# Four graph layers on one core: seven half-size products in layers 1 and 2 as well, the neighbour mask in PSUM, and a new issue order

## The chip, the cores and the metric

The kernel runs on one core of a Trainium2 chip. The metric is the device time of one execution in microseconds (us). The kernel before has a median of 3687.53 us over three runs (3678.21 to 3694.46).

## The reference

64 independent graphs of 256 nodes with 512 features each pass through four layers. Each layer normalises the rows, clips them at zero and adds its result to `x`:

```python
for layer in range(4):
    h = maximum(layernorm(x), 0)
    x = x + gnn[layer](h, adj)

# layer 0: q, k (64 wide), v = h @ W;  w = softmax_n(sum_m((q k^T / 8) * adj));   w * v
# layer 1 (8 heads of 64): f = h @ W + b;  e_self, e_neigh = f . a_self, f . a_neigh
#          d = leaky_relu(e_self[i] + e_neigh[j], 0.2) - 1e10 * (1 - adj);  relu(softmax_j(d) @ f)
# layer 2 (8 heads of 64): p = h @ Wp + b;  relu(tanh(adj * (p C^T p^T)) @ p)
# layer 3: q, k, v (512 wide) = h @ W;  w = softmax_n(sum(q * (adj @ k)) * mask / sqrt(512));   w * v
```

All data are float32.

## The kernel before, in words

A graph's 256 nodes lie as two chunks of 128 partitions (node `2p + c` on partition `p`). For each graph about a hundred *steps* are defined by name in `graph(b)`; a step issues from one to sixteen instructions. The class `Plan` sorts the steps of all graphs by `b * PERIOD + TIMES[name]` (the first nine and the last eight graphs have tables of their own, `FIRST` and `LAST`, and the steps that prepare weights have `WEIGHTS`), records them in this order, and ties each instruction to the one recorded before it on its engine. So every engine works in a fixed order, across some six graphs that are under way at once. Only the order on each engine counts; the tables' times are in us, but nothing waits for a time.

Buffers come from pools by `take` and go back by `done`, first in, first out, also in recorded order: eight PSUM banks, 6 `xt`, 3 `adj`, 6 `at`, 2 `all` (twice as large as the others), 2 `negt`, 2 `half`, and 12 `big` ones, to which 4 are added once the weights are ready.

A layer goes like this. Row sums and squares give `rstd` and `shift` (`sx` on ACT, `rs` on DVE, `pw` and `sh` on POOL; layer 0 uses `st`, the statistics instruction of DVE, line 982, in place of sums). `hn` on ACT makes the normalised rows. To transpose them, `sq` transposes 32 x 32 squares on DVE (line 912), `sw` writes them to memory (line 1029), and `ht` reads them back in the other order (line 917), both issued from the SP queue. Then come the products.

- Layers 0 and 3 (`products`, line 1060) make one product of [256 x 512] by [512 x 2w] from **seven products of half size**. POOL makes four sums of blocks of the transposed rows (`sa`, `sb`, lines 1065 to 1073), PE seven products of two matmuls each (line 1081), and DVE adds their results from PSUM (`add_to`, line 1095; `part_of_score`, line 1135). Their weight differences `t0_s`, `t3_s` are made once.
- Layers 1 and 2 use plain products (`rows`, line 906): `fa` and `fb` with 272 and 256 columns, 4 matmuls for each chunk; `xp` with 512 columns. DVE adds the bias and takes the results out of PSUM (`fae` with the copy `ec`, `fbe`, `xe`; lines 1246 to 1257 and 1436).
- Layer 1 then broadcasts the rows `e_neigh` and `e_self` to all partitions through memory (`er`, `enes`, lines 1271 to 1276), takes the maximum of `e_neigh` over the neighbours (`max0` to `max3`, 16 instructions, line 1288; the mask `neg` turned `adj` into -1e10 where there is no edge, line 944), broadcasts it (`mr`, `mb`), and makes the attention for pairs of heads: `ea` (ACT, line 1327), `eg` adds the mask (POOL, line 1334), `eb` subtracts the maximum (DVE, line 1340), `ex` (ACT, line 1346), `po` (PE, line 1358), `eh` and `su` sum up (POOL line 1367, PE line 1381).
- Layer 2: the transposed projection times C (`xc`, line 1461), scores in pairs of banks (`ps`, line 1487), `tv` (DVE, line 1511), `ta` (ACT, line 1518), `py` (PE, line 1501).
- Layer 3: `agg` (PE, line 1550), its copy `ga` (line 1559), then the seven products `g1` to `g7`. `add3` (DVE, line 1570) adds the weighted rows to `x`, and `store` sends them.

## Time and profile before

| | |
|---|---|
| median of three runs | 3687.53 us |
| the profiled execution, its own time | 3695.39 us |
| its span, first to last instruction | 3693.3 us |
| mean granted clock of PE | 0.985 |
| PE busy (matmuls) | 3494.9 us, 95% |
| DVE busy | 3251.5 us, 88% |
| ACT busy | 2415.6 us, 65% |
| POOL busy | 1623.2 us, 44% |
| busy share of the DMA engines | 69% of 16, 785 MB |

In a group of instructions, the line, engine, operation, tiles and shapes come first, then the count; after the first bar the busy time in us and the mean of one in ns; after the second bar the engine's idle time just before such instructions and what ended it. One f32 product of the program stands as two matmul records. In a list of waits each line has the waiting engine and line, what it waited for, the total in us, the number of times and the longest.

### The profile page before, as it was taken

To read this page: it belongs to the slowest core of one execution; us is meant where nothing else is said; L and a number is where in the kernel's file an instruction comes from. 1 tells how busy PE (TensorE), PEld (TensorE's weight loads), DVE (VectorE), ACT (ScalarE), POOL (GpSimd) and SP (SyncE) were. 2 spreads that over 40 slices of the span, in tenths; PEclk is the share of its full clock that TensorE was granted. 3 is DMA by queue.
4 is the path that set the end of the run, shared out by engine and by line. 5 is a ranking of instruction groups with operands and counts; after the bars stand their busy time and mean duration, and the time that the engine had idled before them with its cause. 6 is when DMAs were issued, how large, how long until landed. Compare 5 with 4: busy or idle time off the path is not lost.

```text
span 3693.3 us, 57357 instructions
## 1 busy us (share of the span) xinstructions
PE 3494.9 (95%) x16322; PEld 2031.4 (55%) x16322; DVE 3251.5 (88%) x8558; ACT 2415.6 (65%) x5381; POOL 1623.2 (44%) x1811
## 2 busy tenths in 40 slices
PE   6889999999999999999999999999999999998988
PEld 3555555555555555555555555555555555555544
DVE  6789898999898999999999899899899999898866
ACT  2567666667667667667766767667666766656654
POOL 2454444454444454444454444354444444343441
PEclk8899999999999999999999999999999999999999
DMA  6667666776776777777777777777677777676643
GB/s 192 196 217 218 211 213 199 223 222 217 222 220 211 224 223 221 227 228 217 222 229 211 223 224 212 219 234 214 216 231 219 221 224 221 198 215 190 210 149 120
DMA packets 967467, 785.00 MB, mean 213 GB/s; under 512 B 788912, under 2 KB 859120, under 8 KB 942576
## 3 DMA queue, kind: packets, MB, share of 16 engines
q1 hardware_dynamic: 967152, 781.34, 69.0%
q8 instruction: 132, 2.16, 0.2%
q14 instruction: 183, 1.50, 0.1%
HBM read 511.12 MB, written 270.01 MB: 211 GB/s over the span
## 4 chain that ended last, share of the span: by engine, by line
DVE 32%; PE 24%; DMA 19%; ACT 10%; issue 7%; SPq 6%; POOL 2%; DVEq 0%; ACTq 0%; POOLq 0%
DMA big<-sq_d 9%; DMA sq_d<-big 9%; PE bank L1081 8%; PE bank L906 7%; DVE big L912 6%; DVE big L1095 5%; ACT big L1416 5%; DVE big L1340 4%; PE bank L1358 3%; SPq L917 2%; SPq L1179 2%; DVE big L1163 2%; ACT big L974 2%; DVE bank L1135 2%; PE bank L1487 2%
## 5 line engine op out<-in xcount | busy, mean ns | idle before, releaser
L906 PE MATMUL bank<-w_s,big 128*128 128x256 f32 (+2 forms) x3072 | 956.1, 462 | 48.7 <-DMA big<-sq_d 42.6
L906 PEld LDWEIGHTS bank<-w_s,big 128*128 128x128 f32 x3072 | 604.3, 199 | 435.1 <-issue 281.9
L1081 PE MATMUL bank<-t_s,big 128*128 128x320 f32 (+1 forms) x1536 | 610.1, 528 | 39.2 <-POOL big L1065 31.2
L996 POOL TENSOR_TENSOR rstd<-rstd,power 128x2 f32<-128x2 f32 x256 | 178.9, 699 | 1053.6 <-DVE rstd L990 999.2
L1334 POOL TENSOR_TENSOR big<-big,negt 128x1024 f32<-128x1024 f32 x256 | 605.8, 2389 | 21.6 <-ACT big L1327 18.0
L1288 DVE CUSTOM_DVE_ANT_0 junk<-all,adj 128x256 f32<-128x256 f32 x1024 | 485.9, 475 | 32.2 <-DMA all<-er_d 1.5
L1346 ACT ACTIVATE big<-big 128x1024 f32<-128x1024 f32 x256 | 258.8, 1051 | 389.6 <-DVE big L1340 388.6
L1367 POOL TENSOR_TENSOR half<-big 128x512 f32<-128x512 f32 x256 | 325.2, 1291 | 424.9 <-ACT big L1346 288.9
L1009 ACT ACTIVATE big<-xt,shift,rstd 128x512 f32<-128x512 f32 x512 | 383.4, 805 | 171.4 <-POOL shift L1002 169.2
L912 DVE STREAM_TRANSPOSE big<-big 128x512 f32<-128x512 f32 x640 | 472.6, 774 | 19.4 <-ACT big L1009 18.9
L1327 ACT ACTIVATE big<-all,ec 128x256 f32<-128x256 f32 x1024 | 428.1, 494 | 80.2 <-DMA all<-er_d 76.4
L1095 DVE TENSOR_TENSOR big<-bank,big 128x320 f32<-128x320 f32 (+1 forms) x704 | 393.9, 568 | 35.4 <-PE bank L1081 19.9
L1081 PEld LDWEIGHTS bank<-t_s,big 128*128 128x128 f32 x1536 | 280.6, 194 | 241.9 <-issue 121.3
L1511 DVE TENSOR_TENSOR big<-bank,at 128x512 f32<-128x512 f32 x512 | 318.1, 673 | 48.1 <-PE bank L1487 46.7
L1518 ACT ACTIVATE big<-big 128x512 f32<-128x512 f32 x512 | 294.1, 625 | 85.5 <-DVE big L1511 81.2
L1081 PE MATMUL bank<-w_s,big 128*128 128x320 f32 x1024 | 323.0, 448 | 11.6 <-ACT big L1103 3.8
L1065 POOL TENSOR_TENSOR big<-big 128x256 f32<-128x256 f32 x128 | 110.3, 862 | 502.9 <-DMA big<-sq_d 462.3
L1340 DVE TENSOR_TENSOR big<-big,all 128x1024 f32<-128x1024 f32 x256 | 304.0, 1245 | 1.9 <-DMA all<-m_d 1.5
L974 ACT ACTIVATE big<-xt,sum 128x512 f32<-128x512 f32 x384 | 272.7, 711 | 42.0 <-DVE sum L1226 29.1
L1416 ACT ACTIVATE big<-big,rs 128x64 f32<-128x64 f32 x1024 | 251.5, 333 | 64.0 <-DMA big<-sq_d 51.8
L1487 PE MATMUL bank<-big,big 64*128 64x256 f32 x2048 | 260.0, 392 | 4.8 <-DVE bank L1135 4.3
L1358 PE MATMUL bank<-big,big 128*64 128x256 f32 x2048 | 243.1, 386 | 17.2 <-ACT big L1346 16.7
(119 smaller groups left out, 5300.0 us busy)
## 6 DMA issues: line engine op xcount, KB each, us to landing
sq_d<-big SPq DMA_DIRECT2D x448, 512.0 KB
big<-sq_d SPq DMA_DIRECT2D x1792, 128.0 KB
all<-er_d SPq DMA_DIRECT2D x128, 1024.0 KB
all<-m_d SPq DMA_DIRECT2D x64, 1024.0 KB
xt<-in_x_dram SPq DMA_DIRECT2D x64, 512.0 KB
out_dram<-xt SPq DMA_DIRECT2D x64, 512.0 KB
adj<-in_adj_dram SPq DMA_DIRECT2D x64, 256.0 KB
blocks<-in_adj_dram SPq DMA_DIRECT2D x256, 64.0 KB
```

The lines of the kernel that those rows point to most:

```text
L906: nc.tensor.matmul(p, chunk(ht[:, k], c), w[:, k], start=(k == 0), stop=(k == KC - 1))
L912: nc.vector.transpose(sq.rearrange("p (r k i c) -> p c k r i", r=4, k=KC, c=NC)[:, c], t[:, c])
L974: nc.scalar.activation(g["hn"][:, c, :], g["xt"][:, c, :], AF.Square, scale=-float(D), bias=st["sum"][:, c:c + 1], accum_out=st["ssq"][:, ...
L1009: nc.scalar.activation(g["hn"][:, c, :], g["xt"][:, c, :], AF.Relu, bias=st["shift"][:, c:c + 1], scale=st["rstd"][:, c:c + 1])
L1081: nc.tensor.matmul(p, a()[:, k], w[:, k], start=(k == 0), stop=(k == 1))
L1095: nc.vector.tensor_tensor(out(), g[i][:, :w], old(), OP.add)
L1288: nc.vector.tensor_tensor_reduce(junk, g["en"][:, h, :], g["adj"][:, c, :], 1.0, -BIG, OP.add, OP.max, g["mx"][:, c, h:h + 1])
L1327: nc.scalar.activation(e[:, s, j, :], g["es"][:, h, :], AF.Prelu, bias=st["ec"][:, j, H + h:H + h + 1], alpha=0.2)
L1334: nc.gpsimd.tensor_tensor(e, e, g["negt"][:, None].to_broadcast([P, 2, NC, N]), OP.add)
L1340: nc.vector.tensor_tensor(e, e, g["m"][:, 2 * p:2 * p + 2, None, :].to_broadcast([P, 2, NC, N]), OP.subtract)
L1358: nc.tensor.matmul(po[s * U:(s + 1) * U, p % 2, :], feats[:, j, h * U:(h + 1) * U], e[:, s, j, :], start=(j == 0), stop=(j == NC - 1))
L1416: nc.scalar.activation(normal_rows(2)[:, c, h * U:(h + 1) * U].rearrange("p (a i) -> p a i", a=2), y[:, h // 2, h % 2 * 2:h % 2 * 2 + 2], ...
```

## The change

1. **Seven half-size products in layers 1 and 2.** `features` and `project` are replaced by `products("f", ...)` with halves of 264 columns (`W1`; the 16 columns for `ec` and the 512 features together) and `products("x", ...)` with halves of 256 (`W2`). Nine adds on DVE (`fe1` to `fe9`) put the features together, six (`xe1` to `xe6`) the projection; two products of layer 2 share a bank each where one add can take both. `ec` is copied out of the features by ACT. Weight differences `t1_s`, `t2_s` are made once, on DVE.
2. **The mask in PSUM.** `neg` writes its result to a PSUM bank (`far`), held until the last of the four `max` steps, which read it there.
3. **Broadcasts in halves.** `enes` becomes `en0`, `en1`, `es0`, `es1`, and `mb` becomes `mb0`, `mb1`, of four heads each.
4. **Two shared pools.** `big` has 19 buffers (and the 4 late ones), which `xt` and the halves of `all` now share; 13 `mid` ones serve `adj`, `at`, `negt`, `half`, `blocks`.
5. **Work moved between engines.** Layer 0 takes its sums and squares on ACT (`sm0`, `sx0`) in place of `st0` on DVE. `rs` of all layers and the last part of `softw` (now `softx`) go from DVE to ACT. `add3` is split: ACT scales (`aw3`), POOL adds.
6. **New tables** `TIMES`, `WEIGHTS`, `FIRST`, `LAST`, and a `PERIOD` of 52.8 where 53.0 stood.

```diff
-PERIOD = 53.0
+PERIOD = 52.8
...
-    keep("xt", 6, [P, NC, D])
-    keep("adj", 3, [P, NC, N])
-    keep("at", 6, [P, NC, N])
-    keep("blocks", 1, [P, N // S, S * NC])
-    keep("all", 2, [P, H, N])
-    keep("negt", 2, [P, NC, N])
-    keep("half", 2, [P, 2, N])
-    keep("big", 12, [P, NC * D])
+    keep("mid", 13, [P, 2 * N])
+    keep("big", 19, [P, NC * D])
...
         @step("neg")
         def _():
-            nc.scalar.activation(g["adj"], g["adj"], AF.Identity, scale=-NEG_BIG, bias=far)
+            far_rows = g.take("bank", 4, name="far").rearrange("p (c n) -> p c n", c=NC)
+            nc.scalar.activation(far_rows, g["adj"], AF.Identity, scale=-NEG_BIG, bias=far)
+            g.done("adj")
...
+        @step("sm0")
+        def _():
+            st["sum"] = small.tile([P, NC], F32, name="sum")
+            for c in range(NC):
+                nc.scalar.activation(normal_rows(0)[:, c, :], g["xt"][:, c, :], AF.Copy,
+                                     accum_out=st["sum"][:, c:c + 1])
...
-                if summed:
-                    nc.vector.tensor_scalar(st["rstd"], st["ssq"], 1.0 / D ** 3, EPS, op0=OP.mult, op1=OP.add)
-                else:
-                    nc.vector.tensor_scalar(st["rstd"], st["mv"][:, :, 1], EPS, None, op0=OP.add)
+                nc.scalar.activation(st["rstd"], st["ssq"], AF.Identity, scale=1.0 / D ** 3, bias=eps)
...
-                nc.vector.tensor_scalar(st["w"], st["w"], st["tot"], None, op0=OP.mult)
+
+            @step(f"softx{layer}")
+            def _():
+                nc.scalar.activation(st["w"], st["w"], AF.Copy, scale=st["tot"])
...
+        products("f", "smf", w1_s[:, :, :W1], t1_s, w1_s[:, :, W1:])
+
+        def part_of_features(name, c, half, rows_in, bank, first=False):
+            @step(name)
+            def _():
+                if first:
+                    g.take("feats", 1 + HP, name=f"feats{c}")
+                nc.vector.tensor_tensor(g[f"feats{c}"][:, half * W1:(half + 1) * W1], g[bank][:, :W1], rows_in(), OP.add)
+                g.done(bank)
...
+        part_of_features("fe1", 1, 0, lambda: b1_bc[:, :W1], "f1", True)
+        part_of_features("fe2", 0, 1, slot(1, 0), "f6", True)
+        part_of_features("fe3", 0, 0, slot(1, 0), "f2")
...
+            nc.vector.tensor_tensor(g["f5"][:, :W1], g["f5"][:, :W1], b1_bc[:, W1:], OP.add)
...
+        part_of_features("fe5", 1, 0, slot(0, 1), "f7")
+        part_of_features("fe6", 1, 1, slot(1, 0), "f5")
+        part_of_features("fe7", 0, 1, slot(0, 1), "f5")
+        part_of_features("fe8", 0, 1, slot(0, 1), "f3")
+        part_of_features("fe9", 1, 0, slot(1, 0), "f4")
...
-        @step("enes")
-        def _():
-            nc.sync.dma_start(g.take("all", 4, name="en"), st["er_d"][H:].partition_broadcast(P))
-            nc.sync.dma_start(g.take("all", HP, name="es"), st["er_d"][:H].partition_broadcast(P))
+        def spread(name, kind, src, users):
+            for q in range(2):
+                def halves(q=q):
+                    @step(f"{name}{q}")
+                    def _():
+                        nc.sync.dma_start(g.take("all", users, name=f"{kind}{q}"),
+                                          src()[q * HA:(q + 1) * HA].partition_broadcast(P))
+                halves()
...
-                    nc.vector.tensor_tensor_reduce(junk, g["en"][:, h, :], g["adj"][:, c, :], 1.0, -BIG,
+                    nc.vector.tensor_tensor_reduce(junk, g[f"n{h // HA}"][:, h % HA, :],
+                                                   g["far"][:, c * N:(c + 1) * N], 1.0, -BIG,
                                                    OP.add, OP.max, g["mx"][:, c, h:h + 1])
...
+        products("x", "smx", w2_s[:, :, :W2], t2_s, w2_s[:, :, W2:])
...
+            nc.vector.tensor_tensor(g.take("xp", 2)[:, 1, :W2], g["xqd"][:, :W2], b2_bc[:, :W2], OP.add)
+            nc.vector.tensor_tensor(xp_row(0), pair_of("xqb"), twice(g["xp"][:, 1, :W2]), OP.add)
+            nc.vector.tensor_tensor(g["xqa"][:, :W2], g["xqa"][:, :W2], b2_bc[:, W2:], OP.add)
+            nc.vector.tensor_tensor(xp_row(1), pair_of("xqa"), twice(g["xp"][:, 0, W2:]), OP.add)
+            nc.vector.tensor_tensor(flat[:, W2:3 * W2], g["xqc"][:, :2 * W2], flat[:, 2 * W2:], OP.add)
+            nc.vector.tensor_tensor(g["xp"][:, 1, W2:], g["xqa"][:, :W2], g["xp"][:, 1, W2:], OP.add)
...
+        @step("aw3")
+        def _():
+            for c in range(NC):
+                u = g["u"][:, 1 - c]
+                nc.scalar.activation(u, u, AF.Copy, scale=st["w"][:, c:c + 1])
...
-                nc.vector.scalar_tensor_tensor(xt, g["u"][:, 1 - c], st["w"][:, c:c + 1], xt, op0=OP.mult, op1=OP.add)
+                nc.gpsimd.tensor_tensor(xt, xt, g["u"][:, 1 - c], OP.add)
```

The issue times in the middle, in us from a graph's zero, before and after:

| step | before | after |
|---|---|---|
| load | -55.958 | -61.473 |
| ht1 (rows for layer 1 read back) | 21.979 | -8.516 |
| first product of layer 1 (fa0; f2) | 22.725 | 3.033 |
| neg | 38.100 | 4.230 |
| max0, max1 | 40.266, 47.890 | 26.441, 32.137 |
| mr, po0 | 70.776, 80.231 | 34.139, 47.145 |
| store | 256.387 | 242.435 |

In the middle of the program, the recorded order after the change has on DVE, next to each other: four maxima, the add that fills `low` (v4), one more add, twelve maxima, the add that frees the bank of v3; and on PE: v4 of layer 0, the `xc` products, v3, `score0`, `agg0` and `agg1`, then the first scores of layer 2, the second of which are written to the bank that v3 had.

## The prediction, made before the changed kernel was run

> **What bounds the kernel now.** I read the page's table of busy time first, then a table of stretches of 400 us, then the groups of instructions with the shapes kept apart, then the timeline of one engine, and the waits last.
>
> The columns of the table of stretches are the stretch, its length, the busy time of the matmul engine (PE), its weight loads, DVE, ACT and POOL, the granted clock, the DMA share and GB/s.
>
> ```profile
> 800.00:1200.00 400.00, 388.53 (x1810) 225.57 (x1809) 360.68 (x964) 273.85 (x612) 181.00 (x206) 0.99 0.72 218
> 1200.00:1600.00 400.00, 393.20 (x1887) 230.03 (x1887) 366.23 (x964) 273.65 (x604) 189.37 (x207) 1.00 0.73 224
> 1600.00:2000.00 400.00, 390.55 (x1867) 228.18 (x1864) 365.98 (x982) 276.76 (x623) 180.85 (x202) 1.00 0.74 223
> ...
> 2400.00:2800.00 400.00, 391.60 (x1829) 228.29 (x1829) 364.67 (x960) 272.84 (x603) 187.21 (x209) 1.00 0.72 222
> ```
>
> In the middle PE is busy about 97.6% of the time, DVE 91%, ACT 68%, POOL 45%. How long is one graph there? The last step of a graph (line 1570, two instructions a graph) tells it, in the view of that line cut to 400 to 3300 us:
>
> ```profile
> L1570 DVE SCALAR_TENSOR_TENSOR xt<-big,w,xt x104: 707/748/1760, 439.2 to 3252.3; 128x512 f32<-128x512 f32 x104
> ```
>
> 104 instructions are 52 graphs; the last start belongs to the second of a pair, so 51 periods take 3252.3 - 0.7 - 439.2 us: **55.15 us a graph**. PE is busy in 53.8 of them and idle in 1.3. A busy PE need not be a PE at its best, so I looked whether its stream is dense (columns: start, length, instructions):
>
> ```profile
> 1894.43 1.89 PE L1081 MATMUL bank<-m_s,big 128*128 128x512 f32 x4
> 1896.15 1.89 PE L906 MATMUL bank<-w_s,big 128*128 128x256 f32 x8
> 1897.88 3.60 PE L1081 MATMUL bank<-wv_s,big 128*128 128x512 f32 x8
> 1901.31 7.03 PE L906 MATMUL bank<-w_s,big 128*128 128x512 f32 x16
> ```
>
> From start to start, 8 records of 256 columns take 1.73 us (0.216 each) and 8 of 512 take 3.43 (0.429). Each f32 product is two records. So half the columns cost half the time, and PE's order is the bound; what PE still waits for is small:
>
> ```profile
> PE bank L906 <- DMA big<-sq_d: 42.6, 29, 15.6
> PE bank L1081 <- POOL big L1065: 31.2, 30, 3.2
> PE bank L1197 <- DVE big L1095: 19.7, 23, 5.6
> PE bank L1358 <- ACT big L1346: 16.7, 16, 2.6
> ```
>
> DVE is close behind. Its waits for others between 400 and 3200 us add up to about 195 us (the largest are 62 for score products and 42 for layer 2's scores, both from PE), 3.8 a graph; the rest of its idle time is small gaps. So it is occupied for 51.3 of 55.15 us.
>
> [...] here the same form differs by 31 ns (line 1135 from PSUM 745, line 961 from SBUF 714). [...] the masked maximum (line 1288) has a median of 424 ns and a mean of 475, and beside POOL work it took 0.71 to 0.84 us.
>
> **The change part by part**, per graph; means are of the whole run, by form.
>
> ```profile
> L1288 DVE CUSTOM_DVE_ANT_0 junk<-all,adj 128x256 f32<-128x256 f32 x1024 | 485.9, 475 | 32.2 <-DMA all<-er_d 1.5
> L982 DVE BATCH_NORM_STATS2 stats<-xt 128x6 f32<-128x512 f32 x128 | 81.9, 681 | 4.3 <-DMA xt<-in_x_dram 4.3
> L1570 DVE SCALAR_TENSOR_TENSOR xt<-big,w,xt 128x512 f32<-128x512 f32 x128 | 93.8, 775 | 1.8
> L1436 DVE TENSOR_TENSOR big<-bank,b_bc 128x512 f32<-128x512 f32 x128 | 86.5, 678 | 14.3 <-PE bank L906 14.3
> L974 ACT ACTIVATE big<-xt,sum 128x512 f32<-128x512 f32 x384 | 272.7, 711 | 42.0 <-DVE sum L1226 29.1 <-DVE xt L961 8.8
> ```
>
> *Products on PE.* Removed are 16 records of 272 columns (229 ns [...], 3.67 us), 16 of 256 (3.45) and 16 of 512 (6.87): 13.99 us. Added are 28 of 264 (222.5 ns, 6.23 us) and 28 of 256 (6.04): 12.27. **PE loses 1.72 us**, all on the path. PE's busy time becomes 52.1.
>
> *DVE.* Out go the statistics of layer 0, the four `rs`, the second half of `softw`, `add3`, and the old copies and adds of `fae`, `fbe`, `xe`: their busy time sums to 490.6 us, 7.67 a graph. In come nine adds of 264 (0.416, between the 407 of 256 and the 477 of 320 columns) and, for layer 2, three of 256 and three of 512 (0.678): 7.00. Net -0.67. The 16 maxima lose at most POOL's share, 51 ns each, [...] I take 31 - 51 = -20 ns, -0.3 us. DVE is then occupied for 50.3 us.
>
> *ACT.* Two sum and two square passes over layer 0 at 0.70 from start to start (lines 974), four `rs` and two `softx` at 0.284 (line 1049), two `ec` at 0.3, two `aw3` at 0.62 (line 1529): 2.8 + 1.1 + 0.6 + 0.6 + 1.2 = 6.3 on top of 37.7. At 44 of 54 us it is hidden; if the cover went, ACT would lack 10 us before it bound. `rs` on ACT stands right behind its square pass, so one hop from ACT to DVE goes (38.8 us of DVE waits in the run); queued behind it are only POOL's `pw` and the next ACT step.
>
> *POOL.* Two more sets of four sums (0.86 + 0.77 + 0.68 + 0.82 = 3.13 each) and two adds of `add3` (1.29 each, line 1367), less 0.34 for the slow `minus` product: +8.5 on 25.4. Behind the four sums wait the mask additions `eg`. At 34 of 54 us it is hidden, but PE waited 31 us in all for such sums in layers 0 and 3, and now there are four sets: up to 0.5 us a graph more, or nothing where `ht` is sent earlier.
>
> *SP and DMA.* The broadcasts in halves move the same bytes with three more issues a graph (0.6 us each, as those of line 917), in a queue that mostly waits: nothing. A half needs one buffer, not a double one, but `xt`, the halves and all else now share 23 buffers where 26 of that size stood, so a load can wait for a buffer. No stall of this kind shows today; 0 to 0.5 us, I take 0.
>
> *PSUM.* The mask holds one bank from `neg` to the last `max`: 4.2 to 32.1 in the issue times. A graph takes 47 banks and not 41. A bank then turns in (8 x 54 - 28) / 46 = 8.8 us, against 8 x 55.15 / 41 = 10.8.
>
> *Order.* In the new order of the middle, DVE does `low` (v4), one more add, then twelve maxima in a row, and only then frees the bank of v3, which PE needs for the scores of layer 2. DVE from v4's landing: 0.9 + 12 x 0.495 (0.465 from start to start in the trace, and 0.03 for PSUM) + 0.45 = 7.3 us. PE in that time: the `xc` products 1.0, v3 1.1, `score0` 1.0, `agg` 3.4: 6.5. PE waits 0.8 us; at 0.44 for a maximum it would be 0.1[...]. Some of today's 1.3 us is of this sort, so I add 0.6.
>
> *Start.* All four parts of the layer-3 weight product now stand ahead of the first graph's products, and DVE makes two more sets of weight differences (about 10 us, once). PE was only 63% busy in the first 100 us, with waits of 6.2 and 15.6 us that may shrink. Between -10 and +20, I take +5.
>
> **Sum.** Period 52.1 + 1.3 + 0.6 = 54.0 us. The span of 3693.3 becomes 3693.3 - 62 x 1.15 + 5 = 3627; there are 63 periods between the first and the last graph's end, and I leave out one for the graphs that fill and drain. The profiled run took 3695.4, 2.1 more than its span and 7.9 more than the median of 3687.5, so on the median's scale it is **3621 us**. In general: 3692.5 - 62 x (55.15 - period).
>
> **Rivals.**
> 1. *The new order also removes waits.* For it: layer-1 products have 11.5 us between `ht1` and the first product in the issue times, 0.7 before, and the longest wait of PE is that one. Against it: only 0.7 us a graph is there. Idle 0.8: period 52.9, 3553 us.
> 2. *DVE takes the gain.* [...] Period about 55.1: 3690 us, no change.
> 3. *Slower: PE waits behind the run of maxima.* Place: the bank of v3. [...] Period 52.1 + 1.3 + 2.8 = 56.2: 3758 us. It decides once new waits of PE exceed 1.72 + 0.3 = 2.0 us a graph. Against it: DVE's work falls.
>
> **How the numbers follow.** The sum 55% (its own range 3584, no new wait, to 3671), rival 1 14%, rival 2 14%, rival 3 17%. The range 3545 to 3705 leaves out most of rival 3 and the edge of rival 1. A measurement of this kernel can tell about 0.5% from no change, that is 3669 to 3706: faster 0.68, same 0.14, slower 0.18.
>
> **What would show it.** PE's busy time near 52 us a graph and idle near 1.9; records of 264 columns at 0.222 us; the maximum's mean at 0.44 to 0.48; DVE's busy share near 91%. Wrong would be: waits of the score products of layer 2 on DVE above 2 us a graph, a maximum above 0.55, waits for buffers in SP's queue, or a start longer by over 20 us.

## The result and the profile after

The changed kernel takes 3693.41 us (median of 20 runs, 3684.92 to 3703.69), the kernel before 3685.16 in the same comparison. The ratio is 1.002, with a 95% interval of 1.0008 to 1.0032. So 3621 us were forecast, and the measured kernel is slower than before by 0.2%. The profiled execution has a span of 3693.2 us.

The same stretches of 400 us as before (columns: stretch, length, busy time of PE, its weight loads, DVE, ACT, POOL, the granted clock, the DMA share, GB/s):

```profile
800.00:1200.00 400.00, 376.32 (x1888) 242.54 (x1888) 368.96 (x939) 315.53 (x739) 256.34 (x276) 1.00 0.73 217
1200.00:1600.00 400.00, 378.96 (x1933) 247.94 (x1935) 367.94 (x927) 316.83 (x739) 257.59 (x273) 1.00 0.74 222
1600.00:2000.00 400.00, 379.85 (x1910) 245.83 (x1906) 367.61 (x923) 312.73 (x739) 258.92 (x281) 1.00 0.74 222
...
2400.00:2800.00 400.00, 379.93 (x1912) 245.88 (x1911) 367.29 (x946) 317.84 (x748) 258.25 (x274) 1.00 0.72 220
```

PE is busy 94.7% of the time where it was 97.6%, and DVE 92% where it was 91%. PE's saving is there, but as idle time. The last step of a graph is now POOL's addition, seen through its line in 400 to 3300 us:

```profile
L1722 POOL TENSOR_TENSOR big<-big,big x106: 1265/1277/1292, 411.2 to 3288.2; 128x512 f32<-128x512 f32 x106
```

106 instructions are 53 graphs, so 52 periods take 3288.2 - 1.3 - 411.2 us: 55.30 us a graph (55.15 before). This stretch takes in the end of the start. For all that follows I use a stretch in the middle, from the store of graph 13 to that of graph 53 in the trace (counted from 1), divided by 40: **54.93 us before, 54.98 after**. Begun a few graphs earlier or later, the same count gives a difference between these two kernels of 0 to 0.3 us, so smaller differences between runs say little. Per graph PE is busy 52.18 us (53.71 before) and waits 2.82 (1.21 before). What PE waits for, between 400 and 3200 us (total, times, longest):

```profile
PE bank L1476 <- ACT big L1464: 62.7, 50, 2.5
PE bank L1131 <- DVE bank L1312: 46.5, 47, 2.5
PE bank L1633 <- DVE mx L1407: 24.6, 44, 1.0
```

In the kernel before, the longest wait and that of the same attention products were, in the same stretch:

```profile
PE bank L1081 <- POOL big L1065: 31.2, 30, 3.2
...
PE bank L1358 <- ACT big L1346: 3.6, 6, 1.2
```

Three of the four waits that the prediction showed are gone, and the fourth, of the attention products for exponentials, has grown from 3.6 to 62.7 us. There are three waits now, one of each in nearly every graph: the attention products `po` for exponentials (1.38 us a graph), the small transpose `softp0` for DVE's `s0v` (0.89), the scores of layer 2 for a bank that the last maximum frees (0.54). DVE's groups, with the shapes kept apart:

```profile
L1012 DVE STREAM_TRANSPOSE big<-big 128x512 f32<-128x512 f32 x640 | 483.6, 782 | 143.6 <-ACT big L1103 143.5
L1407 DVE CUSTOM_DVE_ANT_0 junk<-big,bank 128x256 f32<-128x256 f32 x1024 | 428.9, 419 | 35.3 <-DMA big<-er_d 4.1
...
L1418 DVE TENSOR_TENSOR mx<-mx,ec 128x16 f32<-128x16 f32 x64 | 60.6, 947 | 0.3
...
L1420 DVE TENSOR_SCALAR mx<-mx 128x16 f32<-128x16 f32 x64 | 29.2, 456 | 2.2
...
L1422 DVE TENSOR_TENSOR mx<-mx 128x16 f32<-128x16 f32 x64 | 27.2, 424 | 2.2
...
L1421 DVE SCALAR_TENSOR_TENSOR mx<-mx 128x16 f32<-128x16 f32 x64 | 22.6, 353 | 2.2
```

The maximum fell from 475 to 419 ns, more than predicted. But four tiny operations that follow the maxima (`mxv`, 16 columns each) are now 350 to 950 ns long. In the kernel before, the same four were:

```profile
L1301 DVE SCALAR_TENSOR_TENSOR mx<-mx 128x16 f32<-128x16 f32 x64 | 15.8, 247 | 2.2
L1300 DVE TENSOR_SCALAR mx<-mx 128x16 f32<-128x16 f32 x64 | 13.8, 215 | 2.2
L1298 DVE TENSOR_TENSOR mx<-mx,ec 128x16 f32<-128x16 f32 x64 | 13.5, 212 | 0.2
...
L1302 DVE TENSOR_TENSOR mx<-mx 128x16 f32<-128x16 f32 x64 | 11.5, 180 | 2.2
```

The timeline of the changed kernel shows one instance (start, length, engine, line, what it does; in brackets idle time and what ended it):

```profile
1851.60 2.35 POOL L1452 TENSOR_TENSOR big<-big,mid 128x1024 f32<-128x1024 f32 x1
...
1852.66 0.48 DVE L1202 TENSOR_TENSOR big<-bank,big 128x320 f32<-128x320 f32 x1
...
1852.89 2.31 PE L1633 MATMUL bank<-big,big 64*128 64x256 f32 x16 [0.83 <-DVE mx L1407]
1853.06 0.92 DVE L1418 TENSOR_TENSOR mx<-mx,ec 128x16 f32<-128x16 f32 x1
...
1853.97 0.85 POOL L1172 TENSOR_TENSOR big<-big 128x256 f32<-128x256 f32 x1
1854.02 0.83 DVE L1420 TENSOR_SCALAR mx<-mx 128x16 f32<-128x16 f32 x1
...
1854.89 0.75 POOL L1173 TENSOR_TENSOR big<-big,big 128x256 f32<-128x256 f32 x1
1855.09 0.59 DVE L1422 TENSOR_TENSOR mx<-mx 128x16 f32<-128x16 f32 x1
...
1856.52 0.43 PE L1131 MATMUL bank<-ident,wc 128*128 128x128 f32 x2 [1.32 <-DVE bank L1312]
```

Each slow DVE operation ends within 0.04 us of the end of a POOL operation (1853.98 and 1853.95, 1854.85 and 1854.82, 1855.68 and 1855.64). In the whole run 128 of these 256 small operations take over 0.3 us, and each of the 128 ends within 0.06 us of the end of a POOL operation. Right behind this chain stands `s0v`, for which PE has waited 1.32 us. At this point that is only a coincidence in time; e12, e16 and e17 test it.

The scores of layer 2 start at 1852.89, while the addition that frees the bank of v3 (line 1202) runs until 1853.14. So this wait is not for v3's bank but for the mask's: followed through `take` and `done` in recorded order, the first of these products writes to the bank that the last maximum frees, the second to that of v3.

### The profile page after: what moved, and what is told of

Same layout as the page of the kernel before. It is cut to its first block, busy times and chain, and to the rows that moved or that the text cites. A ratio compares the mean times of both kernels' runs of the same rounds, so it can differ in the third digit from the quotient of the medians.

```text
span 3693.2 us, 61427 instructions
## 1 busy us (share of the span) xinstructions
PE 3401.5 (92%) x16834; PEld 2175.5 (59%) x16834; DVE 3314.2 (90%) x8248; ACT 2781.7 (75%) x6533; POOL 2270.6 (61%) x2452
## 4 chain that ended last, share of the span: by engine, by line
POOL 22%; DVE 18%; issue 15%; PE 14%; DMA 12%; ACT 7%; SPq 6%; POOLq 0%; ACTq 0%; DVEq 0%
PE bank L1188 9%; DMA big<-sq_d 8%; SPq L1017 5%; DVE big L1458 4%; DVE junk L1407 3%; POOL big L1452 3%; POOL rstd L1092 3%; POOL mid L1487 3%; POOL big L1173 3%; DMA sq_d<-big 3%; POOL big L1172 2%; POOL big L1179 2%; DVE big L1202 2%; DVE big L1012 2%; ACT big L1082 2%
## 5 line engine op out<-in xcount | busy, mean ns | idle before, releaser
L1188 PE MATMUL bank<-t_s,big 128*128 128x264 f32 (+3 forms) x3072 | 978.0, 452 | 8.3 <-DVE big L1657 6.1
L1188 PE MATMUL bank<-w_s,big 128*128 128x264 f32 (+2 forms) x3072 | 850.9, 410 | 45.9 <-DMA big<-sq_d 36.3
L1452 POOL TENSOR_TENSOR big<-big,mid 128x1024 f32<-128x1024 f32 x256 | 604.0, 2370 | 98.6 <-ACT big L1445 89.0
L1103 ACT ACTIVATE big<-big,shift,rstd 128x512 f32<-128x512 f32 x512 | 387.7, 805 | 167.3 <-POOL shift L1098 167.0
L1487 POOL TENSOR_TENSOR mid<-big 128x512 f32<-128x512 f32 x256 | 377.1, 1493 | 138.2 <-ACT big L1464 138.2
L1407 DVE CUSTOM_DVE_ANT_0 junk<-big,bank 128x256 f32<-128x256 f32 x1024 | 428.9, 419 | 35.3 <-DMA big<-er_d 4.1
L1082 ACT ACTIVATE big<-big,sum 128x512 f32<-128x512 f32 x512 | 363.8, 712 | 116.7 <-DVE sum L1333 83.7
L1445 ACT ACTIVATE big<-big,ec 128x256 f32<-128x256 f32 x1024 | 428.8, 496 | 5.4 <-DMA big<-er_d 3.1
L1202 DVE TENSOR_TENSOR big<-bank,big 128x320 f32<-128x320 f32 (+1 forms) x704 | 399.5, 571 | 18.2 <-PE bank L1188 13.7
L1476 PE MATMUL bank<-big,big 128*64 128x256 f32 x2048 | 260.7, 388 | 92.2 <-ACT big L1464 91.9
L1458 DVE TENSOR_TENSOR big<-big,big 128x1024 f32<-128x1024 f32 x256 | 325.2, 1309 | 6.5 <-DMA big<-m_d 6.5
L1657 DVE TENSOR_TENSOR big<-bank,mid 128x512 f32<-128x512 f32 x512 | 319.9, 677 | 5.3 <-PE bank L1633 5.2
L1536 ACT ACTIVATE big<-big,rs 128x64 f32<-128x64 f32 x1024 | 257.4, 334 | 24.5 <-DVE rs L1525 13.2
```

The lines of the kernel that those rows point to most:

```text
L1082: nc.scalar.activation(g["hn"][:, c, :], g["xt"][:, c, :], AF.Square, scale=-float(D), bias=st["sum"][:, c:c + 1], accum_out=st["ssq"][:, ...
L1103: nc.scalar.activation(g["hn"][:, c, :], g["xt"][:, c, :], AF.Relu, bias=st["shift"][:, c:c + 1], scale=st["rstd"][:, c:c + 1])
L1188: nc.tensor.matmul(p, a()[:, k], w[:, k], start=(k == 0), stop=(k == 1))
L1202: nc.vector.tensor_tensor(out(), g[i][:, :w], old(), OP.add)
L1407: nc.vector.tensor_tensor_reduce(junk, g[f"n{h // HA}"][:, h % HA, :], g["far"][:, c * N:(c + 1) * N], 1.0, -BIG, OP.add, OP.max, g["mx"][ ...
L1445: nc.scalar.activation(e[:, s, j, :], g[f"s{h // HA}"][:, h % HA, :], AF.Prelu, bias=st["ec"][:, j, H + h:H + h + 1], alpha=0.2)
```

## The experiments

The first four runs set three theories against each other: DVE's list sets the pace (D), PE's own order still does (P), or something that both kernels load alike (S). From e5 on a loop is the theory: the new order ties PE, DVE, ACT and POOL together so that PE's saved time turned into waits. All figures per graph are from the middle of each run, in us; waits are the idle times that the list of waits counts, and shorter gaps are in neither column. The ratios are to the kernel before, run on the same chip.

| run | us | ratio (95%) | graph | PE busy | PE waits | DVE busy | DVE waits |
|---|---|---|---|---|---|---|---|
| before | 3685.16 | | 54.93 | 53.71 | 1.21 | 50.02 | 3.67 |
| changed | 3693.41 | 1.002 (1.0008 to 1.0032) | 54.98 | 52.18 | 2.82 | 50.54 | 3.32 |
| e1_pe_more | 3878.89 | 1.0516 (1.0493 to 1.0539) | 58.04 | 55.86 | 2.17 | 51.64 | 5.51 |
| e2_dve_more | 3751.96 | 1.0181 (1.0160 to 1.0201) | 55.95 | 52.26 | 3.70 | 51.95 | 2.98 |
| e3_transpose_later | 3795.90 | 1.0297 (1.0273 to 1.0322) | 57.04 | 53.21 | 3.81 | 50.86 | 5.06 |
| e4_plain_layer2 | 3867.08 | 1.0489 (1.0466 to 1.0512) | 58.30 | 54.21 | 4.10 | 48.49 | 8.82 |
| e5_pe_more_g4 | 3756.78 | 1.0216 (1.0201 to 1.0231) | 55.91 | 53.51 | 2.42 | 50.82 | 3.92 |
| e6_shift_on_act | 3767.96 | 1.0245 (1.0228 to 1.0262) | 56.44 | 53.07 | 3.36 | 52.64 | 2.90 |
| e7_mask_in_sbuf | 4235.59 | 1.1516 (1.1498 to 1.1533) | 64.78 | 54.73 | 10.02 | 59.67 | 4.22 |
| e8_add3_on_dve | 3768.02 | 1.0242 (1.0224 to 1.0259) | 55.97 | 52.40 | 3.58 | 51.60 | 3.22 |
| e9_scores_first | 3697.54 | 1.0026 (1.0015 to 1.0037) | 55.06 | 52.86 | 2.10 | 50.60 | 3.45 |
| e10_squares_later | 3696.49 | 1.0022 (1.0012 to 1.0032) | 55.01 | 52.28 | 2.75 | 50.76 | 3.11 |
| e11_v3_before_run | 3706.64 | 1.0055 (1.0034 to 1.0075) | 55.19 | 52.48 | 2.71 | 50.75 | 3.25 |
| e12_small_max_in_psum | 3675.46 | 0.9967 (0.9954 to 0.9980) | 54.75 | 52.86 | 1.79 | 50.84 | 2.83 |
| e13_small_max_no_lock | 3706.66 | 1.0049 (1.0030 to 1.0067) | 54.62 | 52.32 | 2.30 | 49.65 | 3.62 |
| e14_before_mask_psum | 3686.32 | 0.9997 (0.9987 to 1.0006) | 54.77 | 53.39 | 1.36 | 49.02 | 4.47 |
| e15_four_together | 3741.04 | 1.0147 (1.0131 to 1.0164) | 56.10 | 53.58 | 2.47 | 50.09 | 5.06 |
| e16_no_mask_addition | 3593.14 | 0.9745 (0.9731 to 0.9760) | 54.05 | 51.95 | 2.11 | 49.27 | 3.68 |
| e17_pool_writes_only | 3600.40 | 0.9771 (0.9755 to 0.9788) | 53.94 | 51.96 | 1.99 | 49.32 | 3.46 |
| e18_small_max_and_v3 | 3686.44 | 0.9994 (0.9982 to 1.0006) | 55.02 | 52.99 | 1.94 | 50.92 | 2.98 |

### More work for one engine: e1, e2, e5

e1_pe_more issues four products twice.

```diff
+for _ in range(2 if f"{name}{i}" in ("f1", "f2", "f4", "x1") else 1):
     for k in range(2):
         nc.tensor.matmul(p, a()[:, k], w[:, k], start=(k == 0), stop=(k == 1))
```

> The changed kernel, with four half-size products of layers 1 and 2 (f1, f2, f4, x1) issued twice into the same bank: the output stays the same, PE works 4 x 0.44 = 1.76 us more a graph, as much as the change had taken from it. Theory D (DVE, with its waits for the normalised rows, sets the pace, and PE waits 2.8 us a graph for it): the extra work fills PE's waits, at most +0.3 us a graph, 3693 to 3712 us. Theory P (PE sets the pace still, its waits are part of its own round): +1.8 us a graph, about 3802 us. Theory S (a resource that both kernels load alike, the DMA engines or the SP queue, holds the period of 54.9 us): no change, 3693 us.

Measured: PE's busy time grew by 3.68 us, because a product is two matmuls, hence four records of 0.222 us, twice what the expectation reckoned; the graph grew by 3.06.

e2_dve_more repeats three DVE operations: the first addition of the features, the first of the projection, and the transpose of `adj`.

```diff
...
+for _ in range(2):
     nc.vector.tensor_tensor(g["xp"][:, 1, :W2], g["xqd"][:, :W2], b2_bc[:, :W2], OP.add)
```

> The changed kernel, with three DVE instructions of each graph issued twice (fe1, xe1, and the transpose of the neighbour blocks): same output, DVE works 0.37 + 0.34 + 0.62 = 1.33 us more a graph. Theory D: the period grows by nearly all of it, 1.0 to 1.33 us, 3755 to 3776 us. Theory P: DVE has 3.3 us of waits a graph, so up to 0.4 us, 3693 to 3720 us. Theory S: no change, 3693 us.

Measured: DVE +1.41, the graph +0.97.

e5_pe_more_g4 doubles one product of layer 3, in another place of PE's order (the edit of e1 with `"g4"` alone).

> The layer-3 product g4 (four records of 256 columns on its own) is issued twice, so PE does four more records of work, between 0.86 us (256 columns) and 1.72 us (512 columns) a graph, in a stretch where DVE is not waiting for PE. If PE's order still sets the pace, the period grows by all of it: 55.3 becomes 56.2 to 57.0, the time 3750 to 3800 us. If the period is set by a loop through DVE, ACT and POOL in the middle of the layers, PE's later waits (0.9 before the score products of layer 3 or layer 2, 1.3 before the attention products) take it in: 0 to 0.5 us a graph, 3693 to 3725 us, and PE's waits fall by 0.4 to 1.7 us.

Measured: PE +1.33, the graph +0.93, and PE's waits took in only 0.40.

What follows: 83% of e1's addition, 69% of e2's and 70% of e5's come out in the length of the graph. PE's work and DVE's both count, so neither is hidden by the other: P and D fall as single causes, and S falls with them. A saving on PE should then have been worth something, if less work counts as more work does: the question becomes what took it back.

### Parts undone: e3, e4, e6, e7, e8

e3_transpose_later moves two square transposes of DVE behind the operation that followed them.

```diff
-"sq0": -50.991, "sw0": -50.971
+"sq0": -49.63, "sw0": -49.62
...
-"sq1": -9.207, "sw1": -8.536, "ht1": -8.516
+"sq1": -7.92, "sw1": -7.91, "ht1": -7.9
```

> The changed kernel with five issue times of the middle graphs altered and nothing else: the transposes of layer 1 (sq1, and its DMAs) stand after two of the four eb steps on DVE, not after one, and those of layer 0 (sq0) after the last adds of layer 2 and its transposes. In the changed kernel's trace DVE waits 2.4 us a graph in front of these two for the rows hn that ACT makes. Theory D: most of the 2.4 us is filled, 1.5 to 2.0 us a graph less, about 3570 to 3600 us. Theory P: PE's order is the same, so within 10 us of 3693. Theory S: 3693 us.

Measured: slower, outside all three expectations. DVE's wait before the square transposes fell from 2.43 to 0.83, but PE's before `po` rose from 1.38 to 2.21, and DVE then waited 2.0 for `po`.

e4_plain_layer2 puts the plain product back in layer 2 (`x1`, `x2` as two products of 512 columns, two additions, no sums on POOL).

```diff
-products("x", "smx", w2_s[:, :, :W2], t2_s, w2_s[:, :, W2:])
...
+rows(g.take("bank", name=f"xp{c}"), g["ht"], c, w2_s)
```

> The changed kernel with layer 2's seven half-size products put back to the plain product of the kernel before (two products of 512 columns, two adds); all else, the issue times too, stays. PE works 0.83 us more a graph, DVE 2.63 - 1.15 = 1.5 us less, POOL 3.1 us less. Theory D: 1.0 to 1.7 us a graph less, 3590 to 3630 us. Theory P: 0.8 us more, about 3745 us. Theory S: 3693 us.

Measured: the graph +3.32 us, outside all three expectations. DVE's busy time fell by 2.05 us and PE's rose by 2.03, and all that DVE gained turned into waits (3.32 to 8.82). PE's wait before `po` grew to 3.27. Such an undoing prices the part and the disturbed order together, and this run can't part them.

e6_shift_on_act makes the shift of the normalised rows on ACT.

```diff
+nc.scalar.activation(st["mean"], st["sum"], AF.Copy, scale=-1.0 / D)
...
-nc.gpsimd.tensor_tensor(st["shift"], st["sum"], st["rstd"], OP.mult)
-nc.gpsimd.tensor_tensor(st["shift"], st["shift"], share_of, OP.mult)
+for c in range(NC):
+    nc.scalar.activation(st["shift"][:, c:c + 1], st["rstd"][:, c:c + 1], AF.Copy, scale=st["mean"][:, c:c + 1])
```

> The shift of the normalised rows is made on ACT, by one small operation on the sum and two on rstd, in place of two small multiplies on POOL, which DVE's additions with two SBUF inputs hold up (445 ns, up to 1.2 us, for an operation of 2 columns). The loop theory: hn comes about 1 us earlier in two or more layers, DVE's 2.4 us a graph of waiting before its square transposes fall by about 1 us, PE's wait for the attention exponentials (1.4 us, behind hn on ACT) falls too, and the period falls by 0.5 to 1.5 us: 3600 to 3660 us. If PE's own work or DVE's own list sets the pace, nothing that matters changes: 3685 to 3710 us, with ACT 2 to 3 us a graph busier.

Measured: DVE's wait for the normalised rows fell by 1.19 us as expected, and yet DVE's busy time rose by 2.10: its large additions of the attention (`eb`) from 1309 to 1610 ns, the four small operations from 2.2 to 2.8 us in sum (means of the whole run). With the shift gone from POOL, its other steps must have come to lie beside these; which ones is not shown here. Missed in its result, but it pointed at what DVE and POOL do at the same time.

e7_mask_in_sbuf takes back the mask in PSUM alone.

```diff
-far_rows = g.take("bank", 4, name="far").rearrange("p (c n) -> p c n", c=NC)
-nc.scalar.activation(far_rows, g["adj"], AF.Identity, scale=-NEG_BIG, bias=far)
+nc.scalar.activation(g["adj"], g["adj"], AF.Identity, scale=-NEG_BIG, bias=far)
...
-keep("mid", 13, [P, 2 * N])
+keep("mid", 14, [P, 2 * N])
```

> The mask stays in its SBUF buffer until the last maximum, as in the kernel before, and no bank is held for it (one buffer more in the pool that adj shares). If DVE's contention with POOL on the maxima counts, 16 maxima go back from 419 to about 480 ns and the period grows by 0.5 to 1 us: 3725 to 3755 us. If the gain on the maxima only moved the contention to the small maxima behind them (213 to 976 ns), those fall back by 1.4 us in sum, and the time stays at 3680 to 3710 us. If a bank held for the mask was what delayed PE, the time falls below 3680 us.

Measured: 15% slower, far outside all three expectations. One line says why:

```profile
L1405 DVE CUSTOM_DVE_ANT_0 junk<-big,mid 128x256 f32<-128x256 f32 x1024 | 949.7, 927 | 33.7 <-DMA big<-er_d 2.6
```

In the new order the maxima run beside POOL's additions of the mask (in the changed kernel's trace 507 of the 1024 overlap one), and with both inputs in SBUF one takes 927 ns on average, not 475. In this order the mask in PSUM is worth about 8 us of DVE a graph. And the four small operations are back at 0.7 us a graph in the middle, as in the kernel before (2.0 in the changed one), as the second expectation had it: with the maxima open to POOL again, the small operations are spared.

e8_add3_on_dve takes back the split of the last addition.

```diff
-nc.gpsimd.tensor_tensor(xt, xt, g["u"][:, 1 - c], OP.add)
+nc.vector.scalar_tensor_tensor(xt, g["u"][:, 1 - c], st["w"][:, c:c + 1], xt, op0=OP.mult, op1=OP.add)
```

> The last step of a graph is one DVE operation a chunk again (775 ns each), and neither ACT's scaling nor POOL's addition is there: DVE 1.5 us a graph busier, POOL 2.4 and ACT 1.2 less. If DVE's list sets the pace or stands in the loop, the period grows by 0.7 to 1.5 us: 3735 to 3785 us. If POOL's work is what holds DVE and ACT up (contention on SBUF), the time falls to 3650 to 3690 us. If PE sets the pace, nothing changes: 3685 to 3710 us.

Measured: DVE +1.06, the graph +0.99. It fits e2: DVE's work counts here.

### One wait removed at a time: e9, e10, e11

e9_scores_first takes away PE's wait before `po`.

```diff
-"hn1": -9.689 ... "ta0": 150.563, "py0": 152.622
+"hn1": -9.62 ... "ta0": 148.775, "py0": 151.98
```

> ACT does ta0 (scores of layer 2, ready) ahead of hn1 (the normalised rows of layer 1, waiting for the shift from POOL), and PE does py0, which uses it, ahead of the attention products po2 that wait for exponentials behind hn1. If PE's saved time was turned into this wait by the new order: the 1.38 us of PE before po2 fall to 0 to 0.3, and the period falls by 0.7 to 1.1 us, 3625 to 3650 us. If the wait only shows that another chain (DVE waiting for hn, contention) sets the pace, PE waits as long at another place and the time stays at 3680 to 3705 us.

Measured: that wait fell from 1.38 to 0.56, and PE's busy time rose by 0.68 (in the run the products of line 1476 were busy for 271.0 us where it had been 260.7, with as many records). Graph and time stayed, as the second reading has it, but not for its reason: PE's waits fell, and the time came back as busy time.

e10_squares_later takes away a DVE wait.

```diff
-"sq0": -50.991, "sw0": -50.971
+"sq0": -49.665, "sw0": -49.66
```

> DVE transposes the squares of layer 0 (sq0) after two additions of the layer-2 projection (xe5, xe6) in place of before them, so that it doesn't stand waiting 1.29 us for the normalised rows. If DVE's waits in the loop set the pace: DVE's 2.4 us before square transposes fall to about 1.2 and the period falls by 0.5 to 1.0 us, 3630 to 3665 us. If POOL's shift is only held up longer by these additions (one of them has two SBUF inputs), or PE is what sets the pace, no change or up to 30 us slower: 3685 to 3725 us.

Measured: DVE's wait for normalised rows fell by 1.25 us; 1.0 of it came back before the first additions of the features. No change in time.

e11_v3_before_run removes the other two waits of PE.

```diff
-"v3": -20.298, "vr0": -20.278 ... "softp0": -17.482, "softv0": -17.231
+"v3": -21.39, "vr0": -21.388 ... "softp0": -17.204, "softv0": -17.203
```

> Two steps of order: the product v3 of layer 0 and the addition that frees its bank stand ahead of the run of twelve maxima, and the small transpose softp0 stands behind the product f3 in PE's order, so PE waits neither for the bank nor for s0v. If PE's saved time was turned into these waits: 0.54 and 0.89 us of PE fall to 0 to 0.4 in sum, the period falls by 0.6 to 1.1 us, 3625 to 3660 us. If the loop through DVE, ACT and POOL around the attention of layer 1 sets the pace: PE's wait before po2 grows from 1.38 to over 2 and the time stays at 3680 to 3710 us.

Measured: the wait for the bank fell from 0.54 to 0.18, but the product `f3`, now ahead of `softp0`, waits 1.06 for the same `s0v` on DVE. The reason is in the pool of banks: `f3`, now the first of the two to take one, gets the bank that `s0v` frees, and needs nothing else of it. So the swap passed the bank on with the wait, and whether `f3` with another bank would have run is not shown. Before `po` PE waits 1.42, not over 2, so the time is in the second range, but not by the path named there.

### The small operations: e12, e13, e18, e15

e12_small_max_in_psum puts the second small array, which the last three of them write or read, in the mask's bank. That bank is then held until the last of the four.

```diff
-far_rows = g.take("bank", 4, name="far").rearrange("p (c n) -> p c n", c=NC)
+far_rows = g.take("bank", 5, name="far").rearrange("p (c n) -> p c n", c=NC)
...
-mx, low = g["mx"][:, :, :H], g["mx"][:, :, H:E]
+mx, low = g["mx"][:, :, :H], g["far"][:, :H * NC].rearrange("p (c h) -> p c h", c=NC)
...
+g.done("far")
```

> The second of the two small arrays in the chain of 16-column operations behind the maxima stands in the mask's PSUM bank, so that the last two of the four operations have one SBUF input each. If two SBUF inputs beside POOL's work are what makes them 2 to 4 times as long: 395 and 287 ns (middle of the program) fall to 180 to 250 each, with the two others unchanged DVE gains 0.2 to 0.4 us and the period 0.1 to 0.3: 3675 to 3690 us. If it is only that they sit where POOL is busy, whatever the operands: no change, 3688 to 3698 us.

Measured: three operations fell to 170 to 180 ns, and the time to 3675.46 us: faster than before by 0.3% (0.2 to 0.5). This is the best kernel here that computes all of the reference. PE's wait for `s0v` is gone (0.02). Much was given back at once, though:

```profile
L1459 DVE TENSOR_TENSOR big<-big,big 128x1024 f32<-128x1024 f32 x256 | 365.6, 1466 | 6.1 <-DMA big<-m_d 6.0
...
L1418 DVE TENSOR_TENSOR mx<-mx,ec 128x16 f32<-128x16 f32 x64 | 62.4, 975 | 0.3
...
L1422 DVE TENSOR_TENSOR mx<-mx,bank 128x16 f32<-128x16 f32 x64 | 10.9, 170 | 2.2
```

The four `eb` of a graph went from 1309 to 1466 ns each (in the middle from 1222 to 1451, or 0.9 us a graph, where the three small operations saved 0.55). POOL's additions of the mask went from 2370 to 2540 ns with them, so these probably lie beside each other now. And PE has a new wait before the scores of layer 2, 1.55 us a graph in place of 0.54, between 400 and 3200 us:

```profile
PE bank L1634 <- DVE mx L1422: 36.0, 45, 1.4
PE bank L1634 <- DVE big L1202: 35.4, 37, 1.5
```

Line 1422 is the last small operation. The second of these products now writes to the mask's bank, which this edit holds until then. The wait before `po` fell from 1.38 to 0.11. So this run tests the small operations and a bank held longer together.

e13_small_max_no_lock frees the first small operation as well.

```diff
+def small_far(k):
+    return g["far"][:, k * H * NC:(k + 1) * H * NC].rearrange("p (c h) -> p c h", c=NC)
+@step("ecp")
+def _():
+    nc.scalar.copy(small_far(0), st["ec"][:, :, :H])
...
-nc.vector.tensor_tensor(mx, mx, st["ec"][:, :, :H], OP.add)
+nc.vector.tensor_tensor(mx, mx, small_far(0), OP.add)
...
```

> On top of the run with the small array in PSUM, ACT copies e_neigh's 16 columns into the half of the mask's bank that is free by then (the two maxima of the first chunk come first), so the first of the four small operations has one SBUF input too. If sharing SBUF with POOL is what costs: that operation falls from 980 to about 200 ns, DVE gains 0.7 us more and the period falls by another 0.3 to 0.6 us against that run: 3640 to 3660 us. If POOL's additions then only meet DVE's large additions of the attention (as they did there: 1.21 to 1.45 us each), those grow by as much again and the time stays at 3668 to 3685 us.

Measured: all four are at 163 to 180 ns, DVE is busy 0.89 us less and the graph is shorter by 0.36. The time is not, 3706.66 us, above both ranges expected. PE has a new wait, between 400 and 3200 us:

```profile
PE bank L1642 <- ACT big L1630: 64.1, 43, 2.8
```

That is `xca` on ACT, which now stands behind the added copy that waits for the maxima. PE waits 1.46 us a graph for it. In the first and last graphs I had put the copy just ahead of `mxv`; the first store comes 6 us later than in the changed kernel, and the last eight graphs take 10 us more.

e18_small_max_and_v3 is e12 with the early `v3` of e11.

> The small array in PSUM, and v3 with the addition that frees its bank ahead of the run of twelve maxima (softp0 stays where it was). PE waits 1.55 us a graph before the score products of layer 2 with the small array alone. If this wait is on the path: it falls to under 0.5 and the period falls by 0.5 to 1.0 us, 3615 to 3645 us. If DVE's list sets the pace there: PE's wait turns up before softp0 or the attention products and the time stays at 3665 to 3680 us; the two additions in front of the maxima may also make it slower, up to 3700 us.

Measured: PE waits 1.94 us, all but 0.16 of it before the scores of layer 2: for the last small operation, which frees the mask's bank. Some 10 us slower than e12. A miss.

e15_four_together joins the edits of e9, e10, e11 and e12.

> The four edits together: scores of layer 2 before the attention products, squares of layer 0 after two additions, v3 before the run of maxima with softp0 behind f3, and the small array in PSUM. If several loops of nearly equal length hold the period, so that each edit alone only passed the wait on: the period falls by 0.8 to 1.5 us against the changed kernel, 3600 to 3645 us. If only the sharing of SBUF with POOL counts: as the small array alone, 3665 to 3685 us. If the edits of order hinder each other: 3690 to 3710 us.

Measured: 3741 us, slower than all three readings. With `softp0` behind `f3`, DVE waits 1.72 us for it, and PE waits 1.73 for the mask's bank. That several equal loops only have to be shortened together is not shown by this run.

### The mask alone: e14

e14_before_mask_psum is the kernel before with the mask in PSUM in its middle graphs.

```diff
-"neg": 38.100
+"neg": 40.200
...
+far_rows = g["adj"]
+if middle:
+    far_rows = g.take("bank", 4, name="far").rearrange("p (c n) -> p c n", c=NC)
+nc.scalar.activation(far_rows, g["adj"], AF.Identity, scale=-NEG_BIG, bias=far)
```

> The kernel before with one part of the change alone: in the middle graphs the mask is written to a PSUM bank, by a step moved from 38.1 to 40.2 in the issue times, just ahead of the first maxima. The prediction took 31 - 51 = -20 ns a maximum. If two SBUF inputs beside POOL are what they lose: 475 falls to about 425 ns, DVE gains 0.8 us a graph, and since PE sets most of the pace there, the period falls by 0 to 0.4: 3660 to 3685 us. If the bank that is held, or the later mask, costs more than that: PE waits for banks freed by DVE, 3690 to 3740 us.

```profile
L1295 DVE CUSTOM_DVE_ANT_0 junk<-all,bank 128x256 f32<-128x256 f32 x752 | 315.6, 420 | 22.7
```

Measured: the maximum takes 420 ns and DVE gains 1.0 us a graph, and the time doesn't move (0.9997, 0.9987 to 1.0006). So in the kernel before this gain of DVE was worth nothing, while in the changed one about 70% or more of added DVE work came out (e2, e8). That the bound moved with the order is likely but not shown: this run takes work away and holds a bank, those add work, and no run adds DVE work to the kernel before. The four small operations stay at 0.7 us a graph in this run. So maxima that don't contend are not enough to push POOL's work onto them; the new order belongs to it.

### POOL's part: e16 and e17

e16_no_mask_addition drops POOL's addition of the mask to the attention scores, its largest work.

```diff
-nc.gpsimd.tensor_tensor(e, e, g["negt"][:, None].to_broadcast([P, 2, NC, N]), OP.add)
```

> The changed kernel without POOL's four additions of the mask to the attention scores (this leaves out part of the computation: the neighbour mask in the attention of layer 1). POOL has 9.3 us a graph less, and these are what DVE's small maxima and its large additions meet. If they hold DVE and the loop up: DVE's busy time falls by 1.5 to 2.0 us (the four small operations from 2.0 to 0.8 us, the others nearer to their undisturbed lengths), PE's waits fall to about 1.5, and the period is 53.5 to 54.2 us, 3605 to 3650 us, near what was predicted. If PE's and DVE's orders alone set the pace: 3680 to 3700 us.

Measured: 3593.14 us, below the range expected, and 54.05 us a graph, the predicted period; the first store comes 15 us earlier than in the changed kernel, which is part of the time. But both POOL's time and its use of SBUF are gone. e17_pool_writes_only keeps the first:

```diff
-nc.gpsimd.tensor_tensor(e, e, g["negt"][:, None].to_broadcast([P, 2, NC, N]), OP.add)
+for _ in range(2):
+    nc.gpsimd.memset(e, 0.0)
```

> In place of each of POOL's four additions of the mask (2.37 us, two SBUF inputs) POOL fills the same buffer with zeros twice (an estimate of 2.1 us from the 0.52 us that 512 columns took at the start), so POOL's time and the order of the steps stay, and only its reading of SBUF there goes (this leaves out part of the computation: layer 1's attention scores). If DVE's loss to the shared SBUF is what costs: the four small operations fall from 2.0 to 0.8 us in sum, DVE is 1.1 to 1.3 us a graph less busy and the time is 3595 to 3630 us, as without the additions. If POOL's time in the chain is what costs: 3675 to 3695 us, whatever DVE gains.

Measured: 3600.40 us and 53.94 us a graph, with POOL busy 33.5 us a graph (35.4 in the changed kernel, 26.0 in e16). The small operations in this run:

```profile
L1420 DVE TENSOR_SCALAR mx<-mx 128x16 f32<-128x16 f32 x64 | 18.2, 284 | 2.2
L1421 DVE SCALAR_TENSOR_TENSOR mx<-mx 128x16 f32<-128x16 f32 x64 | 14.5, 227 | 2.2
L1422 DVE TENSOR_TENSOR mx<-mx 128x16 f32<-128x16 f32 x64 | 12.6, 197 | 2.2
L1418 DVE TENSOR_TENSOR mx<-mx,ec 128x16 f32<-128x16 f32 x64 | 11.8, 185 | 0.3
```

And PE's waits between 400 and 3200 us:

```profile
PE bank L1477 <- ACT big L1465: 64.7, 46, 2.0
PE bank L1634 <- DVE mx L1407: 23.5, 44, 0.9
PE bank L1131 <- DVE bank L1312: 2.8, 4, 1.3
```

In the middle, the time that DVE spends on these four fell from 2.0 to 0.7 us a graph; no other DVE group moved by more than 0.2. PE's wait for `s0v` fell from 46.5 to 2.8 us in this stretch, while the waits before `po` and the scores of layer 2 stayed, and the graph shortened by 1.04 us. What cost the time was what POOL's additions of the mask read from SBUF, not POOL's own time: e16 has 7.5 us less of that than e17 and the same graph. That the cost came by way of the four small operations is not tested alone, but they are all that moved on DVE, and the wait right behind them is the one that went.

## Why the prediction was wrong

- **PE's work** was right: 52.18 us (52.1 predicted). In the trace of before the records of 272 columns start every 229 ns (median, 216 for 256 columns and 429 for 512), in that of the changed kernel those of 264 every 223.
- **The step that failed is the sum of waits**, "1.3 + 0.6": 1.9 was forecast, 2.82 measured. It kept the old 1.3 and added 0.6 for v3's bank. The wait behind the maxima is there, 0.54, but for the mask's bank, for whose holding the prediction put no wait. The old 1.2 vanished (0.7 of it for POOL's sums, 0.2 for the rows of the plain products), as rival 1 had it, and 1.38 before `po` took its place: that this term came out is luck. What was missing is the wait of `softp0` for `s0v`, 0.89. Without it, in e17, PE waits 1.99, the graph takes 53.94 (54.0 predicted) and the run 3600 us.
- **Why it was missed**: the term for the maxima ("31 - 51 = -20 ns") treated the collisions with POOL as a property of the maximum. Measured, the PSUM source costs nothing there (419 ns against an undisturbed 424; the 31 came from two means, 745 and 714, the second with collisions in it, up to 2820 ns; the medians are 752 and 687), and the collisions depend on the place: the same maximum with SBUF sources takes 475 in the old place and 927 in the new (e7). With the maxima immune in the new place (427 ns at most, though 869 of the 1024 overlap a POOL operation), POOL's additions fell on the next operations with SBUF inputs, the four of `mxv` (0.6 to 2.0 us a graph), which I had not costed at all.
- **DVE** came out at 50.54 us busy, +0.51, where -0.97 was predicted. Summed in full lengths, as the prediction summed them, the additions cost 7.1 (7.00) and the removals saved 7.8 (7.67), so these terms were right. But neighbouring operations overlap in the trace (1852.66 + 0.48 and 1853.06 above); counted without overlap, 6.3 stand against 6.4, and the gain of 0.67 is nearly gone. The maxima saved 1.2 and not 0.3. Against that stand +1.4 for `mxv`, +0.4 for the additions of layers 1 and 2 to `x` (line 1063) and +0.4 for the square transposes.
- **ACT** (+5.8 for +6.3) and **SP and DMA** (no wait of PE left there) were as costed. **POOL** rose by 10.1 and not 8.5: 1.0 of the rest is the small multiply of the shift (200 to 445 ns), held by DVE (1.18 us beside an `eb`), and another 1.0 the four `eh`.
- **The start** was put at +5; the first store came 27.6 us later (296.9, 269.3 before), which the prediction had listed as a sign of error. PE waited 18.2 us once for the first rows of layer 1 and 21.7 before the first `po`. It isn't why the time stayed: from the store of graph 57 to that of graph 64 the changed kernel needs 286.0 us, not 310.5, which gives 24.5 back. Neither was tested alone.
- **Rival 2** named the time (3690), and was half right: DVE does take the gain, not by its maxima, which got shorter (475 to 419 ns), but through operations that they pushed into POOL's way. **Rival 3** had PE waiting behind the run of maxima, which it does, but by 0.54 us and for the mask's bank; its 2.8 for v3's bank was an estimate of mine. That a maximum gets dearer with its mask in PSUM is not shown by any run here.

What stays open: why the 1.38 before `po` came in the very size of the waits that went, and whether a complete kernel can have the undisturbed `mxv` without paying elsewhere. e12 got 0.5% against the changed kernel (each against the kernel before, not side by side), e13 and e18 lost it again; all of them, and e15, hold the mask's bank through the small operations, so none tries `mxv` alone.

## What to carry to other kernels

When an operation that two engines contend for is made immune, ask which operation stands next in that window, however small it is, and who waits for it: here, by e17, what fell on four 16-column operations cost 1 us of a 55 us period. A contention cost measured in one order is no price for another order (475 ns a maximum in the old one, 927 in the new). Where buffers go round first in, first out, an edit of the order also hands out other buffers: look who frees the one that a step now takes (e11, e12). And before trading work between engines, add a little to each and see what comes out: here 0.7 to 0.9 of each us added to DVE or PE did.

## What the runs showed of the hardware

- A DVE operation of 16 columns took 0.17 to 0.18 us in the changed kernel where no POOL operation overlaps it (68 of 256), and 0.59 to 0.92 beside POOL in three of the four of the instance shown (2.4 at most in the run): each of these ended when POOL's operation did, within 0.04 us. The one-input form of line 1420 is among them (0.83 us). With its output in PSUM (e12) it took 178 ns on average, not 456.
- It works the other way as well: POOL's multiply of 2 columns (line 1097) took 1.18 us beside DVE's `eb` and 0.20 at most in the nine cases with no DVE work beside it.
- PE was slower in the runs where it waits long. In e7 it waits 9.1 us on average before the scores of layer 2 (338.4 us in 37 times between 700 and 3100 us), and a record of these scores takes 493 ns on average in the run; in the changed kernel, with waits of 0.56 us there, 398. The granted clock between 1200 and 1600 us was 0.92 in e7, 0.97 in e4, whose waits before `po` have 3.3 us on average and 4.4 at most, and 1.00 in the changed kernel. No one length of wait goes with it: in the changed kernel the clock was 0.81 on average from 2197 to 2206 us, around a wait of 2.53 us, and 0.79 from 1085 to 1093, around one of 2.02, but 1.00 from 987 to 996, around one of 2.45.
